# Token-major x, block-turned row sums and a layer norm folded behind W, in a fused attention and recurrence kernel

## The chip, the cores and the metric

The kernel runs on one core of a Trainium2 chip. The metric is the device time of one execution in microseconds (us), as the median of several executions. In a profile, PE is TensorE (the matrix array), PEld its weight loads, DVE is VectorE, ACT is ScalarE, POOL is GpSimd, SP is SyncE, which here issues most transfers. All times below are of runs that the record labels fast, that is, none was over 1.5% above the fastest of its kernel.

## The reference, cut to what matters

```python
# x: 8 images of 128 channels x 48 x 48, that is 2304 tokens of 128 channels each
x = x + conv_attention(group_norm(x), Wq, bq, Wk, bk, Wv, bv)   # causal, with 32 position channels
t = to_tokens(x)
t = t + attention(layer_norm(t))       # softmax(h h^T) h : scores are symmetric, no mask
t = t + ffn(layer_norm(t), W, V, gamma, beta)

def ffn(x, W, V, gamma, beta):
    Wx = x @ W.T                       # then batch norm over all 8 x 2304 tokens
    Wx = (Wx - mean) * rsqrt(var + 1e-5) * gamma + beta
    def step(y, wx_t):                 # a recurrence over the 2304 tokens
        y = sigmoid(wx_t + y @ V.T)
        return y, y
    return scan(step, zeros, Wx)
# returned in the layout of x
```

## The kernel before

The kernel works through the images one after another, each in six chunks of 384 tokens, and interleaves three kinds of work by a schedule that is laid down when the program is built. TensorE computes scores (`s`), ScalarE their exponentials (`p`), TensorE the weighted sums (`o`). As the scores of the second attention are symmetric, part of its exponentials are earlier ones turned around: they are stored to DRAM (`e`) and loaded back (`g`). The first attention is called causal below, the second full. All numbers are 32-bit floats. After the eighth image the last stage runs the recurrence (called the scan below) in 96 segments of 24 steps at once, in 3 groups of 32 segments, each with 12 warm-up steps. It adds the residual t2, compares the ends of the segments with the warm-up states ("seams"), and sets a flag that would start a slow general path.

Three places matter here. First, what follows a causal chunk:

```python
def sums():                                   # the softmax denominators
    for g in range(QB):                       # QB = 3 blocks of 128 tokens
        nc.tensor.matmul(tp[:, g:g+1], acc[:, ts(g, P)], ones[:, 0:1], start=True, stop=True)
    nc.vector.reciprocal(ri, tp[:, :QB])

def residual():
    to = transposed(o_sb, ...)                # three TensorE transposes each
    tx = transposed(xbuf[b][:, cols], ...)    # x_t in the profile
    nc.scalar.copy(xr, tx[:, :QC])
    # ... y = to * ri + xr, on VectorE
```

Second, what follows a chunk of the full attention (t2 is the result in token rows):

```python
def keep():
    tp = transposed(c["t2"], ...)             # tk in the profile
    nc.scalar.copy(self.t2c[:, :, ds(s0, SJ)], tp[:, :QC].rearrange("p (s l) -> p l s", l=LS))
    # ... stores to t2_d, ordered by recurrence step l, in pieces of 128 bytes
def back():
    tp = transposed(c["x2"], ...)             # tx in the profile: normalized t2
    nc.scalar.copy(c["xc"], tp[:, :QC])
def statistics():
    nc.tensor.matmul(tp[:, :QC], w1T, c["xc"], start=True, stop=True)
    nc.vector.bn_stats(stats[:, b * NQ + j, :], tp[:, :QC])
    # ... ScalarE copies the product into wx
```

Third, the last stage. The residual add is in place and reads contiguously. GpSimd does it for the steps below 20, VectorE for the last four; in group 0 an accumulating transfer does the steps below 20:

```python
rst = [... tile_pool(bufs=4 if g == 0 else 6) for g in range(G)]      # rings of y tiles
t2s = [rc.tile([P, LS if g else LS - LM, B, SG], ...) for g in range(G)]
# ... in the loop over steps t and groups g: z += V y, y = sigmoid(z), then
r = t2s[g][:, l0 : l0 + TZ] if g else t2s[0][:, l0 - LM : l0 - LM + TZ]
(nc.gpsimd if l0 < LM else nc.vector).tensor_add(r, y[g][:, so + 1 - TZ : so + 1], r)
nc.sync.dma_start(out[g, :, l0 : l0 + TZ], r)
# ... after the loop: off = any seam too large; one matmul; flag
```

Of the kernel before, what the change touches and what calls it, by code (L numbers as in the profile page):

```python
# [3 lines left out]

# [17 lines left out]
NPE = 2 * EMB  # L22
# [524 lines left out]
class Stream:  # L547
# [14 lines left out]
    def then(self, at, ops):  # L562

        for engine, us in ops:
            at = max(at + self.HOP, self.free[engine]) + us
            self.free[engine] = at
        return at + self.HOP
# [33 lines left out]
def fast_path(ctx: ExitStack, tc: tile.TileContext, x, wq, bq, wk, bk, wv, bv, w_ffn, v_ffn, gamma, beta, pe, out, flag):  # L601
# [24 lines left out]
    t2_d = dpool.tile([SEG_GROUPS, P, LS, B, SG], F32, tag="t2_d", name="t2_d")  # L626
# [3 lines left out]

    ident = cpool.tile([P, P], F32, tag="ident", name="ident")
    make_identity(nc, ident)
    ones = cpool.tile([P, P], F32, tag="ones", name="ones")
# [18 lines left out]
    with ExitStack() as actx:  # L652
# [40 lines left out]
        def load_x(b):  # L693
            xbuf[b] = big.tile([P, N], F32, tag="x", name=f"x_{b}")
            for h in range(2):
                nc.sync.dma_start(xbuf[b][:, ts(h, N // 2)], x_v[b, :, ts(h, N // 2)])

        load_x(0)


# [21 lines left out]
        wpT = chunk_tile("t2", "wpT").rearrange("p (j c) -> p j c", j=3)  # L722
        raw = tpool.tile([P, N // 2], F32, tag="t", name="raw")
        wn = [raw[:, ds(j * (C + NPE), C + NPE)] for j in range(3)]
        vn = raw[:, ds(3 * (C + NPE), P)]
        for j, (w, bias) in enumerate(((wq, bq), (wk, bk), (wv, bv))):
            nc.scalar.dma_start(wn[j], w)
            nc.scalar.dma_start(wpT[NPE : NPE + 1, j, :], bias.rearrange("(o c) -> o c", o=1))
            if j == 0:
                nc.scalar.dma_start(pe_sb[0][: NPE + 1, :], pe[:, : N // 2])  # L730
        nc.scalar.dma_start(pe_sb[1][: NPE + 1, :], pe[:, N // 2 :])
        nc.scalar.dma_start(w1, w_ffn)
        nc.scalar.dma_start(vn, v_ffn)
        nc.scalar.dma_start(gb[:, 0:1], gamma.rearrange("(c o) -> c o", o=1))
        nc.scalar.dma_start(gb[:, 1:2], beta.rearrange("(c o) -> c o", o=1))
        for j in range(3):
            tp = psum_t(f"tp_w_{j}")
            nc.tensor.transpose(tp[:, 0:P], wn[j][:, 0:C], ident)
            nc.tensor.transpose(tp[0:NPE, P : 2 * P], wn[j][:, C : C + NPE], ident)
            nc.vector.tensor_copy(wT[:, j, :], tp[:, 0:P])  # L740
            nc.vector.tensor_copy(wpT[0:NPE, j, :], tp[0:NPE, P : 2 * P])

        def ffn_weights():
            tp = psum_t("tp_ffn")
            nc.tensor.transpose(tp[:, 0:P], w1, ident)
            nc.tensor.transpose(tp[:, P : 2 * P], vn, ident)
            nc.vector.tensor_copy(w1T, tp[:, 0:P])
            nc.vector.tensor_copy(vT_f, tp[:, P : 2 * P])


        SQ = 32
        R = P // SQ
        same = apool.tile([P, R, SQ], F32, tag="same", name="same")
        nc.vector.tensor_reduce(same[:, 0, :], ident.rearrange("p (a c) -> p c a", c=SQ), AX.X, ALU.add)
        for r in range(1, R):
            nc.vector.tensor_copy(same[:, r, :], same[:, 0, :])
        mine = apool.tile([P, NQ - 1, R, QB], F32, tag="mine", name="mine")
        nc.vector.tensor_reduce(mine[:, 0, :, 0], ident.rearrange("p (a c) -> p a c", c=SQ), AX.X, ALU.add)
        for i in range(NQ - 1):
            for g in range(QB):  # L760
                if i + g:
                    nc.vector.tensor_copy(mine[:, i, :, g], mine[:, 0, :, 0])
# [45 lines left out]
        pos = {}  # L808

        def load_positions(b, n):  # L810
            if 0 < b < B:
                pos[b, n] = pbp.tile([P, 3, QC], F32, tag="pb", name=f"pb_{b}_{n}")
                nc.sync.dma_start(pos[b, n], posb_d[:, n])

        def project(b, n):
# [4 lines left out]
            def positions(j):  # L820
                def f():
                    if j == 0:
                        c["pb"] = pbp.tile([P, 3, QC], F32, tag="pb", name=f"pb_{b}_{n}")
                    pe_c = pe_sb[n // (NQ // 2)][: NPE + 1, ts(n % (NQ // 2), QC)]
                    ps = psum_s(f"pb_{n}_{j}")
                    if j < 2:
                        nc.tensor.matmul(ps[:, :QC], wpT[: NPE + 1, j, :], pe_c, start=True, stop=True)
                    else:
                        for m in range(0, QC, P):
                            nc.tensor.matmul(ps[:, ds(m, P)], pe_c[:, ds(m, P)], wpT[: NPE + 1, j, :], start=True, stop=True)  # L830
                    nc.scalar.copy(c["pb"][:, j, :], ps[:, :QC])
                    if j == 2:
                        nc.sync.dma_start(posb_d[:, n], c["pb"])

                return f

            def normed():
                if b:
                    c["pb"] = pos.pop((b, n))
# [5 lines left out]
                c["xn"] = chunk_tile("xn", f"xn_{b}_{n}", c, 4 if b else 7)  # L845
                nc.vector.tensor_scalar(c["xn"], xbuf[b][:, cols], mg, rs, ALU.subtract, ALU.mult)

            def part(j):
                def f():
# [14 lines left out]
                    if j < 2:  # L864
                        nc.vector.tensor_reduce(
                            largest[b][:, j, n : n + 1], dst, AX.X, ALU.max, apply_absolute_value=True
                        )
                    else:
                        load_positions(*divmod(b * NQ + n + 2, NQ))
                        if n + 1 < EARLY:  # L870
                            project(b, n + 1)

                return f

            steps = [] if b else [(positions(j), QC * US, [("ACT", 0.5)]) for j in range(3)]
            steps.append((normed, 0.0, [("DVE", 0.75)]))
# [31 lines left out]
        def transposed(src, name):  # L908
            tp = psum_t(name)
            for g in range(QB):  # L910
                nc.tensor.transpose(tp[:, ts(g, P)], src[:, ts(g, P)], ident)  # L911
            return tp

# [5 lines left out]
        class Causal:  # L919
# [57 lines left out]
            def after(self, j, o):  # L977
# [4 lines left out]
                o_sb = chunk_tile("o", f"oc_{b}_{j}", c, 2)  # L982
                nc.scalar.copy(o_sb, o[:, :QC])
                at = st.then(st.now, [("ACT", 0.5)])

                def sums():

                    tp = psum_t(f"dn_{b}_{j}")
                    for g in range(QB):
                        nc.tensor.matmul(tp[:, g : g + 1], acc[:, ts(g, P)], ones[:, 0:1], start=True, stop=True)  # L990
                    ri = small.tile([P, QB], F32, tag="ric", name=f"ric_{b}_{j}")
                    nc.vector.reciprocal(ri, tp[:, :QB])  # L992
                    c["ri"] = ri

                def residual():
                    to = transposed(o_sb, f"oc_t_{b}_{j}")
                    tx = transposed(xbuf[b][:, cols], f"x_t_{b}_{j}")
                    xr = chunk_tile("xr", f"xr_{b}_{j}", bufs=1)
                    nc.scalar.copy(xr, tx[:, :QC])  # L999
                    y = t1p.tile([P, QC], F32, tag="t1t", name=f"t1t_{b}_{j}")  # L1000
                    for g in range(QB):
                        nc.vector.scalar_tensor_tensor(  # L1002
                            y[:, ts(g, P)], to[:, ts(g, P)], c["ri"][:, g : g + 1], xr[:, ts(g, P)], ALU.mult, ALU.add
                        )
                    if j == NQ - 1 and b + 1 < B:
                        load_x(b + 1)
# [14 lines left out]
                def back():  # L1021
# [4 lines left out]
                    (sums, 0.6, [("DVE", 0.2)]),  # L1026
                    (residual, 0.7, [("ACT", 0.5), ("DVE", 2.6)]),
# [5 lines left out]
        class Full:  # L1033
# [3 lines left out]

            def __init__(self, b):
# [3 lines left out]
                self.used = 0  # L1042
# [23 lines left out]

            def prefetch(self):
                n = len(self.loaded)
# [4 lines left out]
            def turned(self, j, m, p, ready):  # L1073
# [3 lines left out]
                if g == 0:  # L1077
                    self.tiles[n] = tpool.tile([P, R, QB, QB, SQ], F32, tag="t", name=f"t_{b}_{j}_{n}")
# [5 lines left out]
                if g == QB - 1:  # L1084
                    d = dpool.tile([P, R, QB * QB * SQ], F32, tag=f"e_{j}_{n}", name=f"e_{b}_{j}_{n}")
                    nc.sync.dma_start(d, t.rearrange("p b j m r -> p b (j m r)"))
                    self.stored[j, n] = d, at
# [8 lines left out]
            def begin(self, j, what, first):  # L1096
# [12 lines left out]
                if what[0] == "turned":  # L1109
                    i, g = what[1:]  # L1110
                    while (i, j) not in self.loaded:
                        self.load()
# [24 lines left out]
            def after(self, j, o):  # L1137
# [5 lines left out]
                at = st.then(st.now, [("ACT", 0.5)])  # L1143

# [23 lines left out]
                def residual():  # L1168
                    tp = transposed(o_sb, f"of_t_{b}_{j}")
                    t2 = chunk_tile("t2", f"t2_{b}_{j}", c, 5)  # L1170
# [5 lines left out]
                    c["mv"], c["ve"] = moments(t2, f"f{b}_{j}", "l2")  # L1176

                def rooted():
                    c["rs"] = root(c["ve"], f"f{b}_{j}", "l2")

                def normed():
                    c["x2"] = chunk_tile("x2", f"x2_{b}_{j}", c, 6)
                    normalize(c["x2"], c["t2"], c["mv"], c["rs"])

                def keep():
                    tp = transposed(c["t2"], f"tk_{b}_{j}")

                    g, s0 = divmod(j * SJ, SG)
                    if s0 == 0:
                        self.t2c = work1.tile([P, LS, SG], F32, tag="t2c", name=f"t2c_{b}_{g}")  # L1190
                    nc.scalar.copy(self.t2c[:, :, ds(s0, SJ)], tp[:, :QC].rearrange("p (s l) -> p l s", l=LS))
                    if s0 + SJ == SG:
# [219 lines left out]
```

## Time and profile before

| | before |
|---|---|
| time, median of 3 runs (lowest to highest) | 1856.66 us (1853.53 to 1858.67) |
| span of the profiled execution | 1852.4 us |
| granted clock of TensorE, mean | 0.993 |
| first pass of the last stage (a one-row matmul, `pw<-bound`) | 1785.53 us |
| from there to the end | 66.9 us |

The prediction below shows the busy shares, the chain and the waits. Three more views are needed for comparison. The first is the table of windows for one image (window, length, then busy us and instructions of PE, PEld, DVE, ACT and POOL, granted clock, DMA share, GB/s), with the first 20 us of the run as the second row.

```profile
353.47:570.90 217.43, 217.14 (x826) 137.96 (x826) 145.15 (x380) 90.06 (x231) 20.54 (x31) 1.00 0.39 109
0.00:20.00 20.00, 9.59 (x24) 5.82 (x25) 8.03 (x39) 2.72 (x4) 3.01 (x15) 1.00 0.37 117
```

The second is TensorE's timeline of the start (start, length, engine, line, operation, out<-in, shapes, count).

```profile
13.32 2.92 PE L827 MATMUL pb<-pe,wpT 33*128 33x384 f32 x4
...
17.45 2.93 PE L853 MATMUL pj<-xn,wT 128*128 128x384 f32 x4
```

The granted clock is 1.00 there, and still the four passes of the first projection (`pj`) take 2.93 us, twice what later ones take. The third view is of the residual adds (durations in ns: least, median, most; first and last start) and of VectorE's end.

```profile
L1358 POOL TENSOR_TENSOR t2s<-y,t2s x20: 1269/2016/3352, 1810.6 to 1837.1; 128x512 f32<-128x512 f32 x20
...
L1358 DVE TENSOR_TENSOR t2s<-y,t2s x6: 679/1187/1747, 1836.0 to 1843.9; 128x512 f32<-128x512 f32 x6
```

```profile
1841.53 0.40 DVE L1332 TENSOR_TENSOR d<-y,warm 128x248 f32<-128x248 f32 x1
...
1845.97 0.21 DVE L1369 TENSOR_SCALAR flag<-pw,fl 1x1 int32<-1x1 f32 x1 [0.28 <-PE pw L1368]
```

The adds are the last large work. A seam difference (`d`) takes 0.40 us once GpSimd has finished. The flag comes at 1845.97, 6.4 us before the end.

### The profile page before, as it was taken

How to read it: one execution, taken by the hardware profiler on the slowest of the kernel's cores; microseconds unless marked ns; L12 is line 12 of the kernel's file. 1: busy time of each engine (PE TensorE's matmuls, PEld its weight loads, DVE VectorE, ACT ScalarE, POOL GpSimd, SP SyncE). 2: the span in 40 equal slices, each digit the busy share in tenths (PEclk: the TensorE clock that was granted, in tenths of full speed). 3: DMA queues.
4: the chain of work that ended last, by engine and by line, in shares of the span. 5: the costliest groups of instructions: out<-in, count | busy, mean ns of one | idle time of the engine just before them, and what ended most of it. 6: DMA issues, size and time to landing. Idle time of an engine off the chain costs nothing.

```text
span 1852.4 us, 22328 instructions
## 1 busy us (share of the span) xinstructions
PE 1817.4 (98%) x6885; PEld 1159.6 (63%) x6886; DVE 1218.8 (66%) x3152; ACT 773.5 (42%) x1976; POOL 198.4 (11%) x292
## 2 busy tenths in 40 slices
PE   7999999999999999999999999999999999999987
PEld 4666666666666666666666666666666666666656
DVE  5747667575766667575675757666675756757457
ACT  2345334443345423454244433454234542445346
POOL 1100011000110001100110001100011000200006
PEclk9999999999999999999999999999999999999988
DMA  2105551256303571055511563034720456005667
GB/s 92 51 1 192 155 131 35 79 164 175 76 19 128 152 185 48 1 186 143 150 35 57 159 182 95 22 117 148 190 58 1 165 155 158 9 13 166 181 197 206
DMA packets 176558, 207.24 MB, mean 112 GB/s; under 512 B 85865, under 2 KB 147948, under 8 KB 175662
## 3 DMA queue, kind: packets, MB, share of 16 engines
q1 hardware_dynamic: 174608, 202.42, 37.5%
q0 software_dynamic: 720, 2.62, 0.9%
q8 instruction: 57, 0.93, 0.2%
q10 hardware_dynamic: 1102, 0.68, 0.1%
q14 instruction: 71, 0.58, 0.1%
HBM read 112.49 MB, written 93.19 MB: 111 GB/s over the span
## 4 chain that ended last, share of the span: by engine, by line
PE 96%; DVE 1%; POOL 1%; DMA 1%; issue 1%; ACT 0%; SPq 0%; POOLq 0%; DVEq 0%
PE s L1117 18%; PE o L1131 18%; PE s L948 16%; PE o L959 16%; PE o L1127 13%; PE pj L853 3%; PE pj L856 2%; PE wx L1205 2%; PE dn L990 1%; PE x_t L911 1%; PE tb L911 1%; PE of_t L911 1%; PE tx L911 1%; PE oc_t L911 1%; PE z L1346 1%; PE tk L911 1%
## 5 line engine op out<-in xcount | busy, mean ns | idle before, releaser
L1119 ACT ACTIVATE p<-s,shift 128x384 f32<-128x384 f32 x504 | 293.1, 582 | 448.5 <-PE s L1117 435.4
L1117 PE MATMUL s<-xh 128*128 128x384 f32 x1008 | 410.8, 489 | 0.0
L1131 PE MATMUL o<-p,xhT 128*128 128x384 f32 x1008 | 403.2, 487 | 0.0
L948 PE MATMUL s<-q,k 128*128 128x384 f32 (+2 forms) x1008 | 380.2, 459 | 0.5 <-DVE k L863 0.5
L959 PE MATMUL o<-p,vT 128*128 128x384 f32 (+2 forms) x1008 | 377.0, 456 | 0.0
L950 ACT ACTIVATE p<-s 128x384 f32<-128x384 f32 (+2 forms) x504 | 231.0, 462 | 349.6 <-PE s L948 287.4
L1127 PE MATMUL o<-g,xhT 128*128 128x384 f32 x720 | 279.7, 488 | 0.1
L1131 PEld LDWEIGHTS o<-p,xhT 128*128 128x128 f32 x1008 | 188.0, 190 | 121.3
L959 PEld LDWEIGHTS o<-p,vT 128*128 128x128 f32 x1008 | 188.5, 190 | 114.6 <-issue 0.3
L1117 PEld LDWEIGHTS s<-xh 128*128 128x128 f32 x1008 | 183.7, 190 | 106.8
L974 DVE TENSOR_TENSOR acc<-acc,p 128x384 f32<-128x384 f32 (+2 forms) x408 | 210.1, 515 | 60.0 <-ACT p L950 38.1
L948 PEld LDWEIGHTS s<-q,k 128*128 128x128 f32 x1008 | 178.6, 191 | 88.8 <-DVE acc L974 1.1
L1080 DVE STREAM_TRANSPOSE t<-p 128x384 f32<-128x384 f32 x360 | 187.0, 553 | 45.5 <-ACT p L1119 42.7
L1127 PEld LDWEIGHTS o<-g,xhT 128*128 128x128 f32 x720 | 132.2, 190 | 79.0 <-issue 0.7
L1090 DVE TENSOR_REDUCE tsum<-t 128x12 f32<-128x1152 f32 x120 | 162.3, 1353 | 4.1
L858 DVE TENSOR_TENSOR z<-pj,pb 128x384 f32<-128x384 f32 x144 | 79.2, 550 | 110.2 <-PE pj L853 105.3
L953 POOL TENSOR_TENSOR p<-p,triu 128x128 f32<-128x128 f32 x144 | 72.0, 500 | 447.3 <-ACT p L950 446.4
L901 POOL TENSOR_TENSOR rs_f<-ve_f,mhalf 128x3 f32<-128x3 f32 x48 | 41.5, 865 | 684.7 <-DVE ve_f L895 684.7
L992 DVE RECIPROCAL ric<-dn 128x3 f32<-128x3 f32 x48 | 8.5, 177 | 135.9 <-PE dn L990 135.9
L1119 ACT ACTIVATION_READ_ACCUMULATOR p<-s,shift 128x1 f32 x504 | 97.3, 193 | 0.0
L1002 DVE SCALAR_TENSOR_TENSOR t1t<-oc_t,ric,xr 128x128 f32<-128x128 f32 x144 | 41.6, 344 | 68.3 <-ACT xr L999 67.9
L853 PE MATMUL pj<-xn,wT 128*128 128x384 f32 x192 | 80.3, 504 | 0.0
(249 smaller groups left out, 1595.0 us busy)
## 6 DMA issues: line engine op xcount, KB each, us to landing
e<-t SPq DMA_DIRECT2D x120, 576.0 KB, 3.2
g<-e SPq DMA_DIRECT2D x480, 144.0 KB, 3.7
pb<-posb_d SPq DMA_DIRECT2D x42, 576.0 KB, 3.8
x<-in_x_dram SPq DMA_DIRECT2D x16, 576.0 KB, 4.8
out_dram<-t2s SPq DMA_DIRECT2D x26, 256.0 KB, 3.9
t_d<-t2c SPq DMA_DIRECT2D x16, 384.0 KB, 4.4
t2s<-t_d SPq DMA_DIRECT2D x6, 1024.0 KB, 6.9
posb_d<-pb SPq DMA_DIRECT2D x6, 576.0 KB, 2.8
```

Source lines behind the costliest of these rows:

```text
L853: nc.tensor.matmul(ps[:, :QC], wT[:, j, :], xn, start=True, stop=True)
L911: nc.tensor.transpose(tp[:, ts(g, P)], src[:, ts(g, P)], ident)
L948: nc.tensor.matmul(s[:, off:QC], keys[b][:, ts(m, P)], queries[b, j][:, off:], start=True, stop=True)
L950: nc.scalar.activation(p[:, off:], s[:, off:QC], AF.Exp, scale=SCALE)
L959: nc.tensor.matmul(o[:, off:QC], vals[b][:, ts(m, P)], p[:, off:], start=first, stop=last)
L974: nc.vector.tensor_add(a[:, off:], a[:, off:], p[:, off:])
L1080: nc.vector.transpose(t[:, :, :, g, :].rearrange("p b j r -> p j b r"), p.rearrange("p (j b r) -> p j b r", j=QB, b=R))
L1090: nc.vector.tensor_reduce(self.tsum[j][:, n - j - 1, :], t.rearrange("p b j m r -> p (b j) (m r)"), AX.X, ALU.add)
L1117: nc.tensor.matmul(s[:, :QC], xh[:, ts(m, P)], xh[:, ts(j, QC)], start=True, stop=True)
L1119: nc.scalar.activation(p, s[:, :QC], AF.Exp, bias=shift, accum_out=self.rows[:, m, j : j + 1])
L1127: nc.tensor.matmul(out_ap, xhT[:, QB * i + g, :], p, start=first, stop=last)
L1131: nc.tensor.matmul(o[:, :QC], xhT[:, what[1], :], p, start=first, stop=last)
```

## The change

The intent is to relieve TensorE of every transpose that another unit can do. x is also passed in token order. The denominators are made by VectorE. t2 is turned in 32x32 blocks by VectorE and put in place by transfers, so that W multiplies the raw t2 and the product is scaled by 1/deviation behind it. t2 stays in token order in DRAM, which makes the transfers' pieces longer (384 bytes instead of 128), but the last stage then finds its residual in steps of 24 floats. Token order also takes more of SBUF in the last stage, so the rings of y tiles become shorter and the output tiles are three deep. The start gets weights that are already transposed and twelve dummy matmuls.

```diff
 # after a causal chunk
+                y = t1p.tile([P, QC], ...)
+                nc.sync.dma_start(y, x_tok[b, j])
+                def turn():
+                    nc.vector.transpose(ta, acc)
+                    nc.vector.tensor_reduce(c["parts"], ta.rearrange("p (k c) -> p k c", c=SQ), AX.X, ALU.add)
                 def sums():
-                    for g in range(QB):
-                        nc.tensor.matmul(tp[:, g : g + 1], acc[:, ts(g, P)], ones[:, 0:1], ...)
-                    nc.vector.reciprocal(ri, tp[:, :QB])
+                    nc.tensor.matmul(tp[:, :k], same..., c["parts"], start=True, stop=True)   # 12 columns
+                    # ... VectorE: mask, reduce, reciprocal
-                    tx = transposed(xbuf[b][:, cols], f"x_t_{b}_{j}")
-                    nc.scalar.copy(xr, tx[:, :QC])
 # after a chunk of the full attention (the last two chunks of image 8 keep the old way)
+                        nc.vector.transpose(c["tt"]..., t2...)
+                def spread():      # 1/deviation and the turned t2 to DRAM, 3 + 4 transfers
+                def fetch():       # t2x back, and 1/deviation broadcast to all partitions
+                def product():
+                    nc.tensor.matmul(tp[:, :QC], w1T, c["t2x"], start=True, stop=True)
+                    nc.vector.tensor_mul(c["scale"], tp[:, :QC], c["scale"])
 # last stage
-        rst = [... bufs=4 if g == 0 else 6 ...]
+        rst = [... bufs=3 if g == 0 else 5 ...]
+        rres = rctx.enter_context(tc.tile_pool(name="rres", bufs=3))
+        t2s = [rc.tile([P, B, SG * LS], ...) for g in range(G)]
+        t2_g = [t.rearrange("p b (s l) -> p l b s", l=LS) for t in t2s]
+        def add_residual(g, l0, yt):
+            engine = nc.gpsimd if l0 < LM else nc.vector
+            r = rres.tile([P, TZ, B, SG], F32, tag=f"r_{l0 < LM}", ...)   # three for each engine
+            engine.tensor_add(r, yt, t2_g[g][:, l0 : l0 + TZ])
+            nc.sync.dma_start(out[g, :, l0 : l0 + TZ], r)
+        for g in range(G):                       # the last step's adds, after off
+            add_residual(g, LS - TZ, y[g][:, TO[g] - TZ :])
+            if g:
+                continue
             # ... the matmul of off, and the flag
 # start
+        for i in range(12):
+            nc.tensor.matmul(tp[:, :P], ident, ident, start=True, stop=True)
+        # ... position products of chunk 0, then of chunk 1 among the group norm's steps
 # ... cut: host layouts, deferred stores, schedule entries
```

> **What bounds the kernel now.** I began with the page's busy shares, because they say which engine could fill the span.
>
> ```profile
> span 1852.4 us, 22328 instructions
> PE 1817.4 (98%) x6885; PEld 1159.6 (63%) x6886; DVE 1218.8 (66%) x3152; ACT 773.5 (42%) x1976; POOL 198.4 (11%) x292
> PE 96%; DVE 1%; POOL 1%; DMA 1%; issue 1%; ACT 0%; SPq 0%; POOLq 0%; DVEq 0%
> ```
>
> TensorE is busy for 98% of the span and carries 96% of the chain that ended last. Busy time could hide slack, so I next asked the merged chain in order of time for one line that recurs in each of the eight images (first column start, second length, both us):
>
> ```profile
> 353.47 0.75 PE s L1117 x2
> ...
> 570.90 0.75 PE s L1117 x2
> ...
> 788.33 0.75 PE s L1117 x2
> ```
>
> The period is 217.43 us twice running. The table of windows, asked for one such period, gives each engine's busy time in it (instructions in brackets), then the granted clock, DMA share and GB/s:
>
> ```profile
> 483.00:700.00 217.00, 216.71 (x824) 137.70 (x823) 145.14 (x380) 90.05 (x231) 20.54 (x31) 1.00 0.39 109
> ```
>
> TensorE (first) is busy for 216.71 of 217.00 us at full clock, VectorE (third) for 145.14. So one image costs what its TensorE instructions cost, and any pass removed there shortens the image, unless another engine takes over. The matmul lengths overlap in the trace (two passes are shown as 0.81 us), so I price by the distance from one start to the next in the timeline of TensorE:
>
> ```profile
> 506.25 0.49 PE L911 MATMUL tk<-ident,t 128*128 128x128 f32 x3
> 506.58 0.49 PE L911 MATMUL oc_t<-ident,oc 128*128 128x128 f32 x3
> ...
> 510.79 0.72 PE L990 MATMUL dn<-ones,acc 128*128 128x1 f32 x6
> 511.37 0.47 PE L948 MATMUL s<-q,k 128*128 128x128 f32 x2
> 511.68 0.81 PE L959 MATMUL o<-p,vT 128*128 128x384 f32 x2
> 512.33 0.81 PE L948 MATMUL s<-q,k 128*128 128x384 f32 x2
> ```
>
> A group of three transposes costs 0.33 us, a softmax denominator (three matmuls of one column) 0.58 us, a full 384-column matmul 0.65 us. Last, who TensorE waits for:
>
> ```profile
> PE pw L1368 <- DVE off L1367: 6.8, 1, 6.8
> PE tp_w L738 <- DMA raw<-in_L_conv_Wq_dram: 5.4, 1, 5.4
> PE tx L911 <- DVE x L906: 2.5, 1, 2.5
> PE x_t L911 <- ACT t2c L1191: 2.1, 7, 0.3
> ```
>
> Nearly all waiting is at the two ends: weights at the start, the flag at the end.
>
> **What the Trainium skill says.** "Perfetto Trace Analysis", section "Identifying the Most-Contended Engine", warns that matmul busy share is a poor measure of headroom because matmuls are pipelined. The trace agrees (0.81 us shown, 0.65 us apart), hence start-to-start prices. "TensorE: Matmul & The Clock Gate", Part 1, says the array runs at half clock until some 3.4 us of sustained work. The trace agrees: four projection passes at 17.45 us last 2.93 us, later ones about 1.4. "SBUF — State Buffer", section "SBUF: two separate sides", says VectorE and GpSimd lock each other out of a shared port pair; the residual adds of the last stage take GpSimd 1.27 us at best and 2.02 at the median, and VectorE 1.19 at the median against 0.68 at best. "GPSIMD Engine Reference", section 7, puts reads stepping over more than 8 bytes at about +50% per element; nothing in this trace shows such a read in GpSimd.
>
> **The change, part by part.** x arrives also in token order, so the transposes x_t go: 48 groups x 0.33. t2 and its normalized form are no longer transposed by TensorE (tk, tx): VectorE turns 32x32 blocks, DMA places the blocks, and W multiplies the raw t2, whose product is scaled by 1/deviation afterwards (the mean is removed by centring W's rows). The last two chunks of the last image keep the old way, so 46 groups of each go. With 0.325 us: 15.6 + 15.0 + 15.0 = 45.6 us. The denominator becomes one VectorE transpose, a reduce, and one 12-column matmul, which I put at 0.20 us (a third of the old triple): 48 x 0.38 = 18.2 us. Sum off TensorE: 63.8 us, all of it in stretches where TensorE is the limit. By image this is 18 x 0.325 + 6 x 0.38 = 8.1, so the period should fall from 217.4 to 209.3 us.
>
> VectorE gains work, beside TensorE. Per causal chunk: transpose 0.55 (row t<-p, 0.553), reduce 0.55 (row largest, 0.553), two small operations 0.33: 1.43. Per full chunk: transpose 0.55, the roots' turn 0.13 (estimate), scaling out of PSUM 0.55 (row z, 0.550), less three normalizations 0.87 (41.8 us over 48): +0.36. Times six: +10.7, so 145.1 becomes about 156 of 209 us an image, 75%. ScalarE loses two copies of 0.48 per chunk and some of a third. DMA gains four passes over 9.4 MB (x by tokens, t2 out and back, scale in; the old t2 store goes): about 235 MB instead of 207, still some 131 GB/s, and pieces of 128 bytes become 384 or larger. None of this is on the path.
>
> At the start, weights come already transposed, twelve dummy matmuls warm the array, and the position products of the first two chunks fill the wait for x. Before, x had landed by 7.3 us, but the first projection started at 17.45, behind weight transposes (last at 10.39), group-norm steps and a cold position product (13.32 to 17.45). I expect about 11.5: x near 7, statistics 8.4, two small matmuls with VectorE and GpSimd steps to 11. That is 6 us, 2 more for cold passes and 2 for the second chunk's positions; VectorE then becomes the limit for some 10 us (a projected chunk costs it about 5), so I count 8 in all.
>
> At the end, attention's tail and the scan are the same (1776 to 1839 us). Three residual adds leave the path to the flag, of which I count about -2. Against that the residual now is read in steps of 24 floats, into separate output tiles three deep, with shorter rings for y. GpSimd has no slack there, as its timeline shows:
>
> ```profile
> 1830.34 6.12 POOL L1358 TENSOR_TENSOR t2s<-y,t2s 128x512 f32<-128x512 f32 x4
> 1835.25 2.05 POOL L1361 DMA_DIRECT2D out_dram<-y  x1
> 1835.86 4.59 POOL L1358 TENSOR_TENSOR t2s<-y,t2s 128x512 f32<-128x512 f32 x2
> ```
>
> It ends near 1840.4, having worked without a gap. If one strided input of two costs a quarter (estimate from the page's +50%), 20 adds cost 20 x 0.5 = 10 us, of which some 5 would show behind the flag's tail. Landings of 3.9 us (median) with three tiles are borderline as well. I put the end at +4 net.
>
> Sum: 1856.7 - 63.8 - 8 + 4 = 1788.9. I add 3 for new short stalls of TensorE in the eight images: 1792.
>
> **Rivals.** First, VectorE takes over. Its mean says no, but its work comes in lumps: counting the built instructions from the first score matmul of causal chunk 1 to that of chunk 4 and pricing each from its row, it has 34.8 us beside 40.8 of TensorE before and 38.8 beside 39.2 after. Before, chunk 2 alone stood at 13.3 beside 12.2 without a visible stall, since the six p tiles and early projections absorb it; 39 us at the edge could cost 1 to 3 us an image: 1800 to 1815. Second, the round trip of t2 through DRAM is late, or its queue waits hold back the loads of the turned exponentials: TensorE would wait at wx or o. For it speaks that SyncE issues in order and gets nine more issues a chunk; against it, that the schedule allows 10 + 9 us where landings took 3 to 5, and issuing 144 transfers at about 0.35 us is 50 us of 209. It would give some 1800. Third, the last stage is GpSimd's: +10 to +12, 1800. Fourth, all new work hides, the start gives 10 and the end costs nothing: 1780.
>
> **Range and chances.** The 63.8 us are counted and priced from the trace; even half of the start's gain and the two worst rivals together leave it near 1815, still over 2% (below 1819.5). I say 1778 to 1808; faster 0.94, same 0.05, slower 0.01.
>
> **What will show it.** The period of the score line of the full attention should be 209 to 210.5 us; TensorE's share stays at 97% or more; the groups x_t are gone, and tk and tx keep six transposes each; the first projection starts at 11 to 13 us. VectorE's busy time should rise by about 90 us in all. If the period is over 212, look for TensorE waiting on q, k, xn or p (VectorE) or on g, t2x, scale (DMA). At the end, GpSimd's adds above 2.3 us would confirm the stride cost. The prediction is wrong if removed transposes had lain in gaps, which the 0.3 us of idle time an image speaks against.

## The result, and the profile after

The changed kernel takes 1806.0 us (median of 4; 1805.92 to 1807.01) against 1856.96 (median of 4) of the kernel before. The ratio is 0.9729, with a 95% interval from 0.9712 to 0.9746. Ratios here are the mean time of one kernel's fast runs over that of the other's of the same rounds, so they are not quite the ratio of the medians. The page of the profile after begins so; the third line is the chain that ended last:

```profile
span 1804.1 us, 21863 instructions
...
PE 1756.3 (97%) x6291; PEld 1102.3 (61%) x6291; DVE 1301.1 (72%) x3321; ACT 747.1 (41%) x1852; POOL 218.4 (12%) x305
...
PE 95%; DVE 2%; DMA 1%; issue 1%; ACT 0%; POOL 0%; SPq 0%; DVEq 0%; ACTq 0%; POOLq 0%
```

TensorE still carries the chain, and VectorE's share in it has doubled from 1% to 2%. The chain in order of time, and the windows of one image and of the start, answer to those of before:

```profile
361.89 0.75 PE s L1166 x2
...
571.19 0.75 PE s L1166 x2
...
780.49 0.75 PE s L1166 x2
```

```profile
361.89:571.19 209.30, 208.68 (x747) 129.91 (x748) 154.39 (x405) 86.76 (x215) 21.84 (x31) 1.00 0.45 132
0.00:20.00 20.00, 17.78 (x61) 12.95 (x61) 7.69 (x18) 4.15 (x7) 6.08 (x28) 0.74 0.44 152
```

An image takes 209.30 us, twice running, and TensorE is busy for 208.68 of them. In the first 20 us it is granted only 0.74 of its clock. TensorE's waits (in total, times, longest, in us) are these:

```profile
PE pw L1495 <- DVE off L1490: 11.5, 1, 11.5
PE o L1180 <- ACT p L1168: 4.4, 7, 0.6
PE tx L937 <- DVE x L924: 4.1, 2, 2.5
...
PE o L1176 <- DMA g<-e: 0.8, 1, 0.8
```

The wait for the seams at the end grew from 6.8 to 11.5 us. The other waits shown are small. In the last stage ScalarE also waits once for a y tile that an accumulating transfer still reads, and TensorE stops behind it for 3.0 us:

```profile
ACT y L1472 <- DMA out_dram<-y: 3.4, 1, 3.4
```

The start:

```profile
6.55 1.52 PE L827 MATMUL pb<-pe,wpT 33*128 33x384 f32 x4
...
9.80 1.64 PE L827 MATMUL pb<-pe,wpT 33*128 33x384 f32 x2
11.37 0.58 PE L805 MATMUL gn_v<-gn_e,grp 128*128 128x1 f32 x2
...
14.74 2.93 PE L869 MATMUL pj<-xn,wT 128*128 128x384 f32 x4
```

Four position passes (`pb`) take 1.52 us at 6.55, behind the dummies, but two of them take 1.64 us at 9.80, and the first projection is again at the slow 2.93. Last, the adds and VectorE's end:

```profile
L1458 POOL TENSOR_TENSOR r<-y,t2s x20: 1516/1804/2713, 1744.9 to 1785.9; 128x512 f32<-128x512 f32 x20
L1458 DVE TENSOR_TENSOR r<-y,t2s x6: 1416/1688/2755, 1773.5 to 1794.7; 128x512 f32<-128x512 f32 x6
```

```profile
1784.24 3.71 DVE L1450 TENSOR_TENSOR d<-y,warm 128x248 f32<-128x248 f32 x1
1784.39 3.27 POOL L1458 TENSOR_TENSOR r<-y,t2s 128x512 f32<-128x512 f32 x2
...
1791.86 1.44 DVE L1458 TENSOR_TENSOR r<-y,t2s 128x512 f32<-128x512 f32 x1 [2.22 <-DMA out_dram<-r]
1793.21 0.20 DVE L1496 TENSOR_SCALAR flag<-pw,fl 1x1 int32<-1x1 f32 x1
1793.34 2.76 DVE L1458 TENSOR_TENSOR r<-y,t2s 128x512 f32<-128x512 f32 x2
```

A seam difference now takes 3.71 us while GpSimd's last adds run beside it. The add in front of the flag waits 2.22 us for an output tile, and two adds follow the flag. I used the one-row matmul that opens the last stage as a mark to divide the time:

| in the profiles, us | before | after | difference | predicted |
|---|---|---|---|---|
| eight images and start, up to the mark | 1785.53 | 1718.63 | -66.9 | -63.8 - 8 + 3 = -68.8 |
| the mark to the end | 66.9 | 85.5 | +18.6 | +4 |
| span | 1852.4 | 1804.1 | -48.3 | -64.8 |

The first score pass of the full attention in the first and in the last image divides the first row further, before and then after:

```profile
130.16 0.81 PE L1117 MATMUL s<-xh 128*128 128x384 f32 x2
...
1652.18 0.49 PE L1117 MATMUL s<-xh 128*128 128x384 f32 x1
```

```profile
121.11 0.81 PE L1166 MATMUL s<-xh 128*128 128x384 f32 x2
...
1586.21 0.49 PE L1166 MATMUL s<-xh 128*128 128x384 f32 x1
```

It comes 9.05 us earlier in the first image. Five denominators and five groups `x_t` fall out before it, which at the prediction's prices are 3.5 us, so the start itself gave about 5.5. The seven periods between gave 7 x 8.13 = 56.9. From the last image's first score to the mark only 0.9 us were gained, where the removed passes were priced at 3.3: TensorE's waits there grew from 5.6 to 7.7 us.

So the images gave nearly what was expected, and the last stage took back 18.6 us. Within it, the scan's matmuls reach from first to last over 54.8 us instead of 48.7 (+6.1), from there to the matmul that takes `off` it is 11.5 instead of 6.8 (+4.7), from its start to the flag 3.5 instead of 0.2 (+3.3), and from the end of the flag's operation to the end of the program 10.7 instead of 6.2 (+4.5).

### The profile page after: what moved, and what is told of

Same layout as the page of the kernel before. It is cut to its first block, busy times and chain, and to the rows that moved or that the text cites. A ratio compares the mean times of both kernels' runs of the same rounds, so it can differ in the third digit from the quotient of the medians.

```text
span 1804.1 us, 21863 instructions
## 1 busy us (share of the span) xinstructions
PE 1756.3 (97%) x6291; PEld 1102.3 (61%) x6291; DVE 1301.1 (72%) x3321; ACT 747.1 (41%) x1852; POOL 218.4 (12%) x305
## 2 busy tenths in 40 slices
DMA packets 173461, 242.43 MB, mean 134 GB/s; under 512 B 62001, under 2 KB 142034, under 8 KB 173332
## 4 chain that ended last, share of the span: by engine, by line
PE 95%; DVE 2%; DMA 1%; issue 1%; ACT 0%; POOL 0%; SPq 0%; DVEq 0%; ACTq 0%; POOLq 0%
PE s L1166 18%; PE o L1180 18%; PE s L978 17%; PE o L989 16%; PE o L1176 13%; PE pj L869 4%; PE pj L872 2%; PE wx L1260 2%; PE tb L929 1%; PE oc_t L929 1%; PE of_t L929 1%; PE z L1470 1%; DVE r L1458 0%; PE pb L827 0%; DMA out_dram<-r 0%
## 5 line engine op out<-in xcount | busy, mean ns | idle before, releaser
L983 POOL TENSOR_TENSOR p<-p,triu 128x128 f32<-128x128 f32 x144 | 83.5, 587 | 545.8 <-ACT p L980 434.4
L1235 POOL TENSOR_TENSOR roots<-ve_f,mhalf 128x3 f32<-128x3 f32 x48 | 40.7, 849 | 552.5 <-DVE ve_f L913 552.5
L919 POOL TENSOR_TENSOR rs_c<-ve_c,mhalf 128x3 f32<-128x3 f32 x48 | 46.9, 976 | 245.7 <-DVE ve_c L913 245.7
L1222 DVE SCALAR_TENSOR_TENSOR t<-of_t,ri,t1t 128x128 f32<-128x128 f32 x144 | 41.5, 344 | 33.2 <-PE of_t L929 33.2
```

What stands on the lines that cost most here:

```text
L983: nc.gpsimd.tensor_mul(p[:, off : off + P], p[:, off : off + P], triu)
```

## The experiments

My theory was that the last stage pays for the strided residual and for the scarce tiles together, and that the removed passes are worth exactly their start-to-start price. The rivals were that a single scarce ring or the order of the flag is the cause, and that the body's gain has another source, or that the start still holds much. Each kernel is the changed one with the edit shown, unless another is named. "Stage" is the stretch from the mark to the end in the profile. Each call ran the kernel before on the same chip; its medians were 1855.37 to 1856.08 us. Times are medians. Five kernels with the same last stage (the changed one, e5, e6, e7 and e11) took 82.2 to 85.5 us in it, the changed one the longest. So up to some 3 us of the stage depend on something other than its own code, and such a difference between two single profiles shows nothing.

### e1_contig: read the residual contiguously (wrong on purpose)

```diff
-        t2_g = [t.rearrange("p b (s l) -> p l b s", l=LS) for t in t2s]
+        t2_g = [t.rearrange("p b (l s) -> p l b s", l=LS) for t in t2s]
```

> The residual is read with 32 floats side by side instead of in steps of 24 floats (wrong values on purpose, same amount of work). Stride theory: the last stage is longer by 18.6 us because each strided add is slow (VectorE 1.42 us against 0.68, GpSimd 1.52 at best against 1.27): 20 x 0.25 on GpSimd and 6 x 0.7 on VectorE come back, 8 to 12 us, about 1796. Ring theory (output tiles three deep, y ring of group 0 three deep): the waits on transfers stay, only the three adds behind the flag get shorter, 2 to 3 us, about 1803.5.

It took 1801.31 us (ratio 0.9704, 0.9687 to 0.9722), with the expected wrong output, between the two expectations. The stage took 79.0 us, 6.5 less than the 85.5. GpSimd's adds fell to 1.26 us at best and VectorE's to 0.67. But now the tiles are what is waited for:

```profile
POOL r L1458 <- DMA out_dram<-r: 7.7, 3, 2.7
DVE r L1458 <- DMA out_dram<-r: 7.4, 1, 7.4
```

The stride costs something, but removing it alone leaves most of the loss, as faster adds run into the three output tiles.

### e2_rres4: one more output tile for each engine

```diff
-        rres = rctx.enter_context(tc.tile_pool(name="rres", bufs=3))
+        rres = rctx.enter_context(tc.tile_pool(name="rres", bufs=4))
```

> Output tiles of the residual four deep instead of three. Ring theory: GpSimd waits less for a tile to be stored (1.65 + about 2 + 2 us of idle time are seen), so its adds end some 4 us earlier: 1801 to 1803. Stride theory: nothing, 1806.

It took 1799.54 us (0.9692, 0.9671 to 0.9712), and the stage 77.6 us. No wait for an output tile is left and the scan runs nearly without a stop (one wait of 0.2 us for a y tile). VectorE now reaches its adds earlier and is held there:

```profile
1770.72 12.01 DVE L1458 TENSOR_TENSOR r<-y,t2s 128x512 f32<-128x512 f32 x3 [0.42 <-ACT y L1472]
1782.65 0.41 DVE L1450 TENSOR_TENSOR d<-y,warm 128x248 f32<-128x248 f32 x1
```

Three adds that take 1.42 us each alone took 12.01 us, until GpSimd's last add ended at 1781.4, and the seam difference after them is back at 0.41. This one number in the source gives 6.5 us by the medians, somewhat more than expected.

### e3_y0ring4: one more y tile for group 0

```diff
-bufs=3 if g == 0 else 5
+bufs=4 if g == 0 else 5
```

> Four y tiles for group 0 as before the change, instead of three. Ring theory: ScalarE's wait of 3.4 us for the accumulating transfer goes, 1802 to 1803. Stride theory: the wait was only a place where slack collected, under 1 us, 1805 to 1806.

It took 1805.27 us (0.9725), which is the time of the changed kernel, and the stage 85.4. VectorE's wait for an output tile grew from 2.2 to 9.3 us:

```profile
DVE r L1458 <- DMA out_dram<-r: 9.3, 1, 9.3
```

So the 3.4 us for which ScalarE had waited for a y tile were only the place where the delay was visible.

### e4_flag_first: the flag ahead of the last adds

```diff
+        nc.tensor.matmul(pw[0:1, P : P + 1], off, ones[:, 0:1], start=True, stop=True)
+        nc.vector.tensor_scalar(flag, pw[0:1, P : P + 1], fl[:, 1:2], 0.5, ALU.add, ALU.is_gt)
         for g in range(G):
             add_residual(g, LS - TZ, y[g][:, TO[g] - TZ :])
-            # ... the matmul and the flag after g == 0
```

> The flag is computed before the last residual add of group 0, which waits for a tile. If the flag ends the kernel: 3 us less, 1803. If the last stores behind the adds end it: within 0.5 us of 1806.

It took 1803.65 us (0.9718, 0.9701 to 0.9735), 2.4 us less by the medians. As a number this is nearer to the first expectation than to the second, though the interval overlaps that of the changed kernel. But in the profile the flag came at 1787.5, the adds still waited 1.98 us for a tile and ended at 1793.8, and the program ended with their stores, at 1800.3. Of the 3.4 us by which the stage was shorter (82.1), 2.0 lie before the place of the edit and 1.4 behind it. So the order of the flag explains little of the 18.6 us.

### e5_dn_old: the old denominators in the new kernel

```diff
-                    # VectorE transpose and reduce, one 12-column matmul, mask, reduce (cut, and the schedule entries)
+                    for g in range(QB):
+                        nc.tensor.matmul(tp[:, g : g + 1], acc[:, ts(g, P)], ones[:, 0:1], start=True, stop=True)
```

> One part undone: the causal denominators again by three one-column matmuls on TensorE, no block transposes and row sums on VectorE. If TensorE is the limit through all images: 48 x 0.38 = 18 us more, 1824, period 211.6 us. If VectorE's new work had already taken part of the gain (the rival): clearly less than 18, below 1818.

It took 1824.95 us (0.983, 0.9814 to 0.9847), 19.0 us more by the medians and 18.7 by the ratios (0.0101 of 1856). The chain shows the period, 366.77 - 154.94 = 211.83 us:

```profile
154.94 0.75 PE s L1156 x2
...
366.77 0.75 PE s L1156 x2
```

The 18.2 us predicted for this part are confirmed, and this period is 2.53 us longer where 6 x 0.38 = 2.3 were priced (the seven periods differ, 211.7 to 212.5).

### e6_old_turn4: four of six chunks by the old transposes

```diff
-                last = b == B - 1 and j >= NQ - 2
+                last = j >= SG // SJ
```

> One part undone for four of six chunks: chunks 2 to 5 of each image go back to TensorE transposes of t2 and of its normalized form, with no round trip through DRAM. Priced as in the prediction: 30 more chunks x 2 x 0.325 = 19.5 us, 1825.5, period 217.4 - 0.33 x 6 x 1 ... in numbers 209.3 + 4 x 0.65 = 211.9 us. If the round trip cost waits: less than 19.5.

It took 1833.43 us (0.9883, 0.9866 to 0.9899), 27 us more, where 19.5 were expected. The period was 213.39 us instead of 211.9. The surplus is a wait:

```profile
PE tx L937 <- DVE x L924: 13.0, 8, 2.5
```

Once an image TensorE waits for VectorE's normalized t2, 13.0 us in all where the changed kernel has 4.1. The 4.4 us for exponentials are gone in this run, so TensorE waits about 4.5 us more than in the changed kernel. With the expected 19.5 that makes 24 of the 27. By the period, 4.09 us were added: 2.6 are the price of the transposes, 0.9 are more idle time of TensorE (1.56 instead of 0.62), and some 0.6 us an image stay unexplained. So this run does not measure the price cleanly. The old way is worse in the new schedule than it was in the old one, where this wait came once.

### e7_no_idle: no dummy matmuls

```diff
-        for i in range(12):
+        for i in range(0):
```

> Without the twelve dummy matmuls at the start. If warming them up pays: 2 to 4 us more, 1808 to 1810. If not, because the array is cold again when the first projection comes at 14.7 us (2.93 us for four passes): within 1 us of 1806.

It took 1806.74 us (0.9741, 0.9725 to 0.9758), so by the time of the whole the dummies are worth 1 to 2 us, within the intervals, which is inconclusive. Up to the mark they are worth 2.3 us (1720.9 instead of 1718.6); this profile's stage happened to be shorter (82.2). Its windows are more telling than its time; the clock is the third number from the end:

```profile
10.00:15.00 5.00, 5.00 (x15) 3.36 (x14) 1.43 (x7) 1.44 (x3) 0.71 (x2) 1.00 0.29 118
15.00:20.00 5.00, 5.00 (x14) 3.26 (x14) 1.74 (x4) 0.96 (x2) 0.47 (x2) 1.00 0.29 118
```

The changed kernel has these:

```profile
10.00:15.00 5.00, 5.00 (x13) 3.07 (x14) 1.08 (x5) 1.11 (x3) 0.57 (x1) 0.50 0.29 118
15.00:20.00 5.00, 4.95 (x13) 2.92 (x13) 3.14 (x6) 0.32 (x1) 0.00 (x0) 0.57 0.29 118
```

Without dummies the first projection starts at 16.79 instead of 14.74, and again takes 2.93 us. Its passes run at half rate from 7.23 to about 21 although the clock is granted fully. With dummies the array is fast from 6.55 to 8.7 and then granted about half its clock. So the dummies bring the position products and the first projection forward by 2 us, and the projection is slow either way.

### e8_fix1: longer rings, group 0's residual kept apart

```diff
+    t2k_d = dpool.tile([P, LS - LM, B, SG], ...)     # the last 4 steps of group 0, ordered by step
-        rst = [... bufs=3 if g == 0 else 5 ...]
-        rres = ... bufs=3
+        rst = [... bufs=4 if g == 0 else 6 ...]
+        rres = ... bufs=6
-        t2s = [... for g in range(G)]
+        t2s = [... for g in range(1, G)]             # 24.6 KB of a partition come free
+        t2k = rc.tile([P, LS - LM, B, SG], ...)      # 4 KB
 # ... its stores and loads
```

> Right results: group 0 keeps its last four steps' residual apart (4 KB a partition instead of 24 KB), and the room goes into rings of 4 (y of group 0), 6 (y of groups 1, 2) and 6 (output tiles). Ring theory: no waits for tiles, the scan runs at TensorE's pace, GpSimd still ends late by its slower adds; 8 to 10 us less, 1796 to 1798. Stride theory: about 2 us less (group 0's two adds no longer strided), 1804.

It is correct and took 1796.48 us (0.968, 0.9664 to 0.9697). The stage took 76.2 us (the profile caught the slowest execution, 1800.44). The trace puts no idle time of an engine down to a tile any more, but GpSimd and VectorE now collide:

```profile
L1465 POOL TENSOR_TENSOR r<-y,t2s x20: 1520/2250/4616, 1747.2 to 1778.6; 128x512 f32<-128x512 f32 x20
L1465 DVE TENSOR_TENSOR r<-y,t2s x4: 1415/2081/2748, 1779.1 to 1789.4; 128x512 f32<-128x512 f32 x4
L1465 DVE TENSOR_TENSOR r<-y,t2k x2: 680/3582/6485, 1772.7 to 1787.3; 128x512 f32<-128x512 f32 x2
```

A contiguous add of VectorE (`r<-y,t2k`) takes 0.68 us alone and took 6.49 beside GpSimd's.

### e9_old_end: the new images with the old last stage

```diff
+    t2o_d = dpool.tile([SEG_GROUPS, P, LS, B, SG], ...)      # ordered by step, as before
-                    if j < SG // SJ:
-                        keep(c["t2x"])
+                    keep(c["t2x"])                            # ScalarE copy of every chunk
+                        nc.sync.dma_start(t2o_d[g, :, n:, b, :], self.t2c[:, n:])
 # last stage: rings 4 and 6, in-place contiguous adds, the flag's order: all as before
```

> The changed kernel with the last stage of the kernel before: residual kept in the scan's own order (pieces of 128 bytes written during attention again, one ScalarE copy per chunk), read side by side, added in place, rings of 4 and 6. Right results. If the whole loss against the prediction lies in the last stage: that stage (from the small matmul on the bounds to the end) takes 67 us as before instead of 85.5, and the time is 1806 - 18.6 = 1787 to 1788. If the pieces of 128 bytes or the extra copies hold up attention: more, up to 1795, and the period is then above 209.3 us.

It is correct and took 1794.9 us (1793.66 to 1795.79; ratio 0.9664, 0.9651 to 0.9677). This is the fastest correct version by the medians, faster than both kernels; the intervals of e2 and e8 overlap with its own. Its stage took 69.2 us, near the 66.9 of before, and its period is the new one, 209.30:

```profile
153.39 0.75 PE s L1167 x2
...
362.69 0.75 PE s L1167 x2
```

It pays on the other side: the mark came at 1723.83, 5.2 us later than in the changed kernel. About 1 us of it was lost at the start. The other 4 arose in the last image, where TensorE waited 2.8 us for exponentials and 2.1 for turned ones (`g`), against 0 and 0.8 in the changed kernel. SyncE stood 15.1 us there at the stores behind ScalarE's extra copy, but in the changed kernel it stood 12.5 us at such a store (`tt`) in the same image. That SyncE's order is the cause is therefore argued and not shown. The short packets (under 512 bytes) rose from 62001 to 115617.

### e10_rings_contig: e8 with contiguous reads as well (wrong on purpose)

```diff
 # on top of e8_fix1
-        t2_g = [t.rearrange("p b (s l) -> p l b s", l=LS) for t in t2s]
+        t2_g = [t.rearrange("p b (l s) -> p l b s", l=LS) for t in t2s]
```

> The kernel with the long rings (1796.5), and the residual read side by side as well (wrong values on purpose). If the strided reads, and the lock between VectorE and GpSimd that they lengthen, are what remains of the loss: the last stage goes from 76.2 to 67 to 69 us, about 1788 to 1790. If something else remains, such as separate output tiles or the larger stores' order: at least 73 us, 1793 or more.

It took 1789.53 us (0.9639, 0.9622 to 0.9655), with the wrong output meant. The stage took 68.6 us:

```profile
L1465 POOL TENSOR_TENSOR r<-y,t2s x20: 1265/1970/2914, 1745.2 to 1772.1; 128x512 f32<-128x512 f32 x20
L1465 DVE TENSOR_TENSOR r<-y,t2s x4: 669/675/1742, 1773.9 to 1780.3; 128x512 f32<-128x512 f32 x4
```

With this, the loss is divided: 85.5 to 76.2 by the tiles (with two of VectorE's six adds made contiguous), 76.2 to 68.6 by the remaining stride, and 1.7 us of the 18.6 stay without a name, which is within the spread of the stage. The separate output tiles are not it: e9 adds in place and takes no less (69.2).

### e11_start: the second chunk's positions behind the first projection

```diff
-        st.advance(gn, 2)
-        positions(1, 0)
         st.finish(gn)
-        for j in range(1, 3):
-            positions(1, j)
         project(0, 0)
+        st.advance(projected[0, 0], 4)
+        for j in range(3):
+            positions(1, j)
```

> The changed kernel with the second chunk's position products moved behind the first projection, so that they don't stand in TensorE's queue between the two group-norm sums at half clock. If they delayed the first projection: it starts at about 12.4 us instead of 14.7, and 1 to 2 us are saved, 1804 to 1805. If VectorE's chain sets the start in any case: the projection starts earlier, but the time stays at 1806.

It took 1811.06 us (0.9755, 0.9738 to 0.9771), 5 us more, where I had expected a small gain or none. The projection came at 12.72 as wanted. But the first score pass of the full attention came at 128.4 instead of 121.1, and the granted clock was low for longer:

```profile
0.00:20.00 20.00, 15.68 (x61) 12.07 (x62) 9.21 (x21) 4.19 (x8) 6.08 (x28) 0.83 0.38 123
20.00:40.00 20.00, 18.50 (x46) 10.05 (x47) 6.61 (x15) 5.10 (x12) 1.36 (x3) 0.59 0.41 148
40.00:60.00 20.00, 18.58 (x70) 11.43 (x71) 12.96 (x27) 5.16 (x12) 1.36 (x3) 0.89 0.37 125
```

The changed kernel has 0.74, 0.91 and 1.00 in these three stretches. TensorE had two new gaps, of 0.79 and 1.42 us, before `gn_v` and before the projection. That the gaps lowered the clock is only argued, and the kernel before speaks against it: TensorE was busy for only 9.59 of its first 20 us, at 1.00. That record is itself doubtful, since passes ran at half rate under it. What sets the granted clock in the first 45 us stays open.

### e12_act_store: e9 with the stores of t2 issued by ScalarE

```diff
 # on top of e9_old_end
-                            nc.sync.dma_start(out[g, :, :n, b, :], self.t2c[:, :n])
-                        nc.sync.dma_start(t2o_d[g, :, n:, b, :], self.t2c[:, n:])
+                            nc.scalar.dma_start(out[g, :, :n, b, :], self.t2c[:, :n])
+                        nc.scalar.dma_start(t2o_d[g, :, n:, b, :], self.t2c[:, n:])
```

> The kernel with the old last stage, its 24 stores of the reordered residual issued by ScalarE, which made the copy, instead of SyncE. In the old-last-stage kernel SyncE stood 15 us at these stores in the last image while loads of turned exponentials waited behind them, and the body was 5.2 us longer than in the changed kernel, about 4 of it in that image. If SyncE's order is the cause: 4 us less, 1791, with the small matmul on the bounds at about 1720 us. If the DMA engines' load with pieces of 128 bytes is: within 1 us of 1795.

It is correct and took 1827.02 us (1817.36 to 1829.67; 0.9853), 32 us more than e9. The profile caught the fastest execution. In it the loads of turned exponentials (`g`) come late, and SyncE waits for stores that ScalarE had issued:

```profile
PE o L1177 <- DMA g<-e: 23.3, 8, 6.1
```

```profile
SPq L1248 <- DMA out_dram<-t2c: 43.7, 8, 9.2
```

Those 23.3 us, against 2.1 in e9, are about the loss of the profiled execution against e9's (span 1815.0 against 1793.0). The other executions are some 10 us longer, with a granted clock of 0.981 to 0.983 instead of 0.989. Whether the stores delay the loads inside the DMA engines or only through SyncE's wait for them, this run does not tell.

## Why the prediction was right or wrong

**What bounds the kernel: right.** TensorE filled an image before and fills it now. The period is the predicted 209.3, the count of removed passes times their start-to-start price. That price, not the 0.49 us that a group of three transposes shows as its length, was the right one. ("Perfetto Trace Analysis", which the prediction found confirmed, says that pipelined instructions look smaller in a trace; here a 384-column pass looks longer, 0.49 us, than the 0.33 us to the next one's start. The conclusion, not to go by busy time, holds.) That it fits to the decimal is partly luck: TensorE's busy time in an image fell by 217.14 - 208.68 = 8.46 us, 0.33 more than priced (the new denominator matmul takes 0.14 us from start to start, not 0.20), and its idle time rose by as much, from 0.29 to 0.62. e5 confirms the denominators alone (18.2 predicted, 18.7 to 19.0 measured by medians; its runs spread over 5.5 us). The transposes of t2 were undone for four chunks of six in e6, which brought a wait of its own, and those of x in no run. They are shown by the period of all of them together.

**VectorE, ScalarE and DMA beside it: right.** VectorE has 154.39 us in an image (156 predicted) and 82 more in all (about 90 predicted). DMA moved 242.43 MB (235 predicted). The first rival, VectorE in lumps, fell (only in the last image TensorE waits longer for it, 4.1 us for `x` instead of 2.5), and so did the second, the late round trip: TensorE waited for exponentials 4.4 us in all, 0.6 once an image, and for `g` 0.8. The 3 us added for stalls came as these 0.6 us an image, which the cheaper denominators made up for, and as some 2.4 us that the tail of the last image fell short of its price.

**The start: the mechanism in part, the size wrong.** The step "I expect about 11.5 ... I count 8 in all" failed. The first projection started at 14.74, 2.7 us earlier and not 6, and the start gave about 5.5 us of the 8. Two terms were mis-sized. The "2 more for cold passes" did not come, because the first projection took 2.93 us as before, now at a granted clock of 0.50 to 0.57. The prediction took these 2.93 us as agreeing with full rate after some 3.4 us of sustained work. They don't: before the change TensorE worked without a gap from 12.80 to 21.66 us, and all of it at half rate (four `pb` passes 2.92 us at 13.32, against 1.55 at 23.13). The projection was also held back by position passes issued around `gn_v`: e11 starts it 2.0 us earlier without them. But e11 is slower as a whole, so this order was not a mistake of the change.

**The end: the mechanism right, the size wrong.** The term "+4 net" measured +18.6, and this is nearly the whole distance between 1792 and 1806. The text had named the stride, three-deep tiles and shorter rings, and its third rival ("The last stage is GpSimd's: +10 to +12, 1800") came nearest: GpSimd's last add ended 69.0 us after the mark instead of 54.9. Four things went wrong in its working.

- It took off 2 us for adds that leave the path to the flag. One add stayed ahead of the flag and waited for a tile, so from the matmul of `off` to the flag it is 3.5 us instead of 0.2.
- It charged the stride to GpSimd, with 0.5 us an add. At best an add rose by only 0.25 us (1.27 to 1.52), and the sign named for the stride cost, adds above 2.3 us, did not appear in the median (1.80).
- It charged nothing to VectorE, whose six adds doubled at their best, 0.68 to 1.42 us, and lie on the last path. The Trainium skill could have warned: "Vector Engine (DVE) Microarchitecture Reference", section 5.2, "Measured stream behaviour on trn2", has 1.054 ns per column for contiguous operands and 2.50 for both sources, or the destination alone, stepping 24 words on every element. It has no row for one such source. Here one source does so, and (1416 - 679) / 512 = 1.44 ns a column were added, near the page's 2.50 - 1.054 = 1.45.
- It called three tiles "borderline" and gave them no price. They cost about as much as the stride: one more tile alone gave 6.5 us by the medians (e2), contiguous reads alone 4.7 (e1). Tiles and rings together, with two adds made contiguous, gave 9.3 us of the stage (e8), and the remaining stride then 7.6 (e10). e3 shows that the y ring of group 0 alone is worth nothing.

Alone, e1 gave 6.5 us of the stage and e2 7.9; both together, with the longer y rings (e10), gave 16.9 of the 18.6. I read the traces as a chain: a late add delays its store, the store the next tile, and the tile an add that then runs beside VectorE's and holds it up. The last link is seen in 0.40 us operations that took 1.74 and 3.71 us while GpSimd's adds ran; the chain as a whole is argued, and only the two causes at its head, stride and tiles, were tested.

**The sum** by the profiles is -63.8 - 5.5 + 2.4 + 18.6 = -48.3 us (passes, start, tail of the last image, last stage), where -64.8 was predicted. The worst case in the prediction was added up too kindly: half of the start's gain (4), VectorE's rival at its worst (1815, that is 23 over 1792) and another rival's 8 make about 1827, above the 1819.5 of a clear gain, not "near 1815". The direction and the range held because the 63.8 us, the part that could be counted, outweighed the two ends, which had only been estimated.

## What to carry to other kernels

Price a removed instruction by its start-to-start distance on the engine that bounds the stage, and the gain in that stage can be known to a few per cent (8.1 us an image priced, 8.46 of busy time here). Then price the stretches at both ends as carefully, operation by operation and for each engine: a data layout that is good for the long stage can double an operation in the short one, where nothing hides it. When the new layout eats the space of buffers, count that as a cost of its own, and try one more tile in each ring first.

## What the Trainium skill lacked or had wrong

- "Vector Engine (DVE) Microarchitecture Reference", section 5.2: it has no row for one source stepping 24 words with the rest contiguous. Measured here: an add of 512 columns takes 1.42 us instead of 0.68 at best, as much more as the page's row for both sources would give.
- "GPSIMD Engine Reference", section 7: +50% per element for reads stepping over more than 8 bytes; it does not say what one of two inputs costs. With one of two stepping 96 bytes, an add here rose from 1.27 to 1.52 us at best, +19%.
- "TensorE: Matmul & The Clock Gate", Part 1: full rate after some 3.4 us of sustained work. The kernel before worked for 8.9 us at half rate (12.80 to 21.66). Without dummy matmuls, TensorE worked from 7.23 to about 21 us without a gap and at half rate, with a granted clock recorded as 1.00; with them it was fast at 6.55 and slow again from 9.80, with 0.50 recorded. In e11 a granted clock of 0.50 to 0.81 lasted to 45 us. The page's two states do not explain which record goes with which rate; the page itself warns that the recorded clock events are unreliable.
- "DMA: Bandwidth & Descriptors", section "Issuing engines are not separate DMA queues": it says that issuing from several engines saves only issue time. It doesn't warn that it can cost: moving 24 + 8 stores to ScalarE (e12) took 32 us more than e9 by the medians, 22 in the profiles. Why is open.
